# Merge of an attention layer without copies by column: stores by image, column blocks made in memory, statistics behind the next sums

## The chip, the cores and the metric

The kernel runs on one core of a Trainium2 chip. A core has TensorE (PE: matrix products, into PSUM), VectorE (DVE), ScalarE (ACT), GpSimd (POOL) and SyncE (SP, which only issues transfers), an on-chip memory of 128 partitions, and 16 DMA engines between it and the chip's main memory. SP and ACT each have a DMA queue. The metric is the time of one execution on the device, in microseconds (us).

## The reference

The input x has the shape 2 x 128 x 128 x 128 (images, channels, rows, columns; 16.8 MB in float32). Four layers follow each other, each as x = x + layer(groupnorm(x)):

- layer 0: axial attention along the rows' axis, for every column, in 8 groups, with relative position embeddings and batch normalisation of the logits and of the output;
- layer 1: four recurrent scans, down, up, right and left. A step is `y = x_i + relu(conv1d(y_prev, w))` with nine taps over 128 channels; the first two scans go over rows, the last two over columns;
- layer 2: a deformable 3 x 3 convolution;
- layer 3: a 4 x 4 convolution with stride 2, done through Hadamard transforms.

For this case the seam between layers 0 and 1 matters. Layer 1's residual is the sum x1 = x + layer0: its scans start from the normalised x1 and overwrite it, and the last scan adds the unnormalised x1 to its result.

## The kernel before, in words

*Preparation* (`layer0_prepare`). Both images are loaded to the chip (`xa`), moments of the logits are gathered, and the projected tensors are written to main memory: `v_d`, then `qa_d` from the tile `sa` and `qb_d` from `sb`. The pool `l0x` that holds the images is given memory from the left end, and so are the pools of `sa` and `sb` after it.

*Attention* (`layer0_attention`). 64 units of one image, one group and 32 columns. Its constants `toep` and its operands `zz`, `qk` and `r` are in pools at the right end. Unit 0 starts with POOL's clearing of the two `zz`, then SP loads 16 pieces of `zz`, then TensorE multiplies them with `toep` into `gen`.

*Merge* (`class Merge`). The attention's two outputs lie in main memory, `sv_d` by column and `sve_d` by row. There are 8 units (2 images of 4 blocks of 32 columns), each of two halves of 16 columns. For a half, `add` lets ACT scale and turn the columns of `tv` into `u`, in two quarters, and DVE sums them into `te`; `to_image` adds `te` to the image x in `res`, POOL the rows 0 to 63 and DVE the rows 64 to 127, and DVE takes four `bn_stats` of the result, first of its own rows, then of POOL's. `by_column` then lets ACT turn each quarter into the tile `bc` and store it, from its own queue, in `x1_d`, which holds x1 by column. SP loads `te`, `tv` and the image, each when a buffer is free. In the pools `InOrder` keeps the order of the text on an engine: ACT's is sums of this half, then columns of the half before; DVE's is sums, addition, statistics.

*Layer 1* (`layer1`). The statistics become a scale and a shift (`group_norm`); ACT starts loads for three further scan weights; `layer3_weights`, called as `prepare`, loads layer 3's weights from ACT's queue, lets POOL form sums of them and stores them from ACT's queue again. Then ACT normalises rows, four ahead of the scan. A scan step is 14 matmuls on TensorE, one ACT copy of a PSUM tile (`c0`), six DVE operations, and two ACT copies (lines 1177 and 1178) that write the new line back to the image, both images in one access. In the fourth scan POOL writes instead: `here = new + add`, where `add` is a line of x1. It comes from the tile `x1t`, eight columns of x1 by column, loaded by `load_columns` from `x1_d`, two blocks ahead. DVE takes statistics of the finished lines right after POOL's additions (`stats`).

The order of instructions on each engine is fixed when the program is built: by the text where `InOrder` is used, by a scheduler elsewhere. An instruction waits on semaphores; the DMAs of SP and ACT share eight of them in turn, so a DMA is also held until the eighth one before it has landed.

Of the kernel before, what the change touches and what calls it, by code (L numbers as in the profile page):

```python
# [15 lines left out]
P = 128  # L16
N = 2
# [74 lines left out]
def layer0_prepare(env, x, prm, mem, alphas):  # L92
# [7 lines left out]
    nc, tc = env.nc, env.tc  # L100
    HW = WC // 2
    with ExitStack() as ctx:
        xpool = ctx.enter_context(tc.tile_pool(name="l0x", bufs=1))
        kp = ctx.enter_context(tc.tile_pool(name="l0k", bufs=1))
        xa = [xpool.tile([P, S, S], F32, name=f"xa{n}", tag=f"xa{n}") for n in range(N)]
        pe, dve, act = (InOrder(tc, e) for e in (nc.tensor, nc.vector, nc.scalar))
# [782 lines left out]
class Merge:  # L889

    def __init__(self, env, x, mem, x1_d, ctx):
        self.env, self.x, self.mem, self.x1_d, self.ctx = env, x, mem, x1_d, ctx
        self.units = [(n, wc) for n in range(N) for wc in range(NC)]
        self.sums, self.embedded = {}, {}
        self.sync = InOrder(env.tc, env.nc.sync)
# [69 lines left out]
    def run(self, prm, res, mv, st_gn):  # L968
        nc, tc = self.env.nc, self.env.tc
        HWC, HS = WC // 2, S // 2  # L970
        act, dve, pool = (InOrder(tc, e) for e in (nc.scalar, nc.vector, nc.gpsimd))
        sp, units = self.sp, self.units
        with ExitStack() as ctx:
            cp = ctx.enter_context(tc.tile_pool(name="mg_c", bufs=1))
            pp = ctx.enter_context(tc.tile_pool(name="mg_ps", bufs=1, space=PSUM))
            for part in range(4):
                self.load_rows(res[0], 0, part)
            a, shift = self.scales(cp, pp, prm, mv)

            def there(at, hf):  # L980
                n, wc = units[at]
                lo = wc * WC + hf * HWC
                return res[n][:, :, lo : lo + HWC]

            HQ = HWC // 2

            def add(at, hf):

                tv = self.sums.pop((at, hf))
                for q in range(2):  # L990
                    u = sp.tile([P, S, HQ], F32, name="u", tag="u")
                    act.activation(
                        u.rearrange("p h w -> p w h"),
                        tv[:, q * HQ : (q + 1) * HQ],
                        AF.Identity,
                        bias=shift,
                        scale=a[:, 0:1],
                    )
                    lo = hf * HWC + q * HQ
                    te = self.embedded[at][:, :, lo : lo + HQ]  # L1000
                    dve.scalar_tensor_tensor(te, te, a[:, 1:2], u, ALU.mult, ALU.add)

            def to_image(at, hf):

                n, wc = units[at]
                te = self.embedded[at][:, :, hf * HWC : (hf + 1) * HWC]
                image = there(at, hf)
                for h, engine in ((0, pool), (HS, dve)):
                    here = image[:, h : h + HS, :]
                    engine.tensor_tensor(here, te[:, h : h + HS, :], here, ALU.add)  # L1010
                for b in (2, 3, 0, 1):
                    dve.bn_stats(
                        st_gn[:, n, wc * NB + hf * 4 + b, :], image[:, b * 32 : (b + 1) * 32, :]
                    )

            def by_column(at, hf):
                n, wc = units[at]
                image = there(at, hf)
                for q in range(2):
                    t = sp.tile([P, HQ, S], F32, name="bc", tag="bc", bufs=3)  # L1020
                    act.copy(t, image[:, :, q * HQ : (q + 1) * HQ].rearrange("p h w -> p w h"))
                    lo = wc * WC + hf * HWC + q * HQ
                    act.dma_start(out=self.x1_d[:, n, lo : lo + HQ, :], in_=t)

            last = None
            for at in range(len(units)):
                for hf in range(2):
                    if at > 0:  # L1030
                        add(at, hf)
                        if at + 1 < len(units):
                            self.load_sums(at + 1, hf)
                    elif hf == 0:
                        for k in range(2):
                            add(0, k)
                            self.load_sums(1, k)
                        self.load_rows(res[1], 1, 0)
                        self.load_rows(res[1], 1, 1)
                    if last is not None:  # L1040
                        by_column(*last)
                    last = at, hf
                    to_image(at, hf)
                if at + 2 < len(units):
                    self.load_embedded(at + 2)
                if at in (0, 1):
                    self.load_rows(res[1], 1, at + 2)
            by_column(*last)

# [9 lines left out]
    return wl, ws  # L1061


def layer1(env, prm, res, both, x1_d, st_gn, st_next, first, prepare):

# [1 line left out]
    nc, tc = env.nc, env.tc  # L1069
    HS = S // 2  # L1070
    with ExitStack() as ctx:
        cp = ctx.enter_context(tc.tile_pool(name="l1c", bufs=1))
        sp = ctx.enter_context(tc.tile_pool(name="l1s", bufs=3))
        with tc.tile_pool(name="l1pn", bufs=1, space=PSUM) as pn:
# [1 line left out]
        pp = ctx.enter_context(tc.tile_pool(name="l1ps", bufs=2, space=PSUM))  # L1076
        weights = [first] + [scan_weights(env, prm, cp, d) for d in range(1, 4)]
        prepare()
        xp = ctx.enter_context(tc.tile_pool(name="l1x", bufs=3))


        lines = [
# [7 lines left out]
            InOrder(tc, e) for e in (nc.tensor, nc.vector, nc.scalar, nc.gpsimd)  # L1090
        )

        CB = 8

        def load_columns(w0):
            t = xp.tile([P, N, CB, S], F32, name="x1t", tag="x1t")
            nc.sync.dma_start(out=t, in_=x1_d[:, :, w0 : w0 + CB, :])
            return t

        def stats(t, n):  # L1100
# [17 lines left out]
        for d in range(4):  # L1118
# [4 lines left out]
            for at, line in enumerate(steps):  # L1123
# [7 lines left out]
                new = [t[:, :, 2 : 2 + HS] for t in now]  # L1131
                if d == 3:
                    w0 = line // CB * CB
                    if line == w0 + CB - 1 and w0 >= 2 * CB:
                        columns[w0 - 2 * CB] = load_columns(w0 - 2 * CB)
                    add = [columns[w0][:, :, line - w0, k::2] for k in range(2)]
                if at == 0:
                    for k in range(2):
                        dve.tensor_copy(new[k], here[k])
# [588 lines left out]
def layer3_weights(env, prm, w3_d):  # L1728
# [5 lines left out]
    with tc.tile_pool(name="l3w", bufs=1) as wp:  # L1734
# [2 lines left out]
        tk = [wp.tile([P, 4, 2, H], F32, name=f"tk{k}", tag=f"tk{k}") for k in range(2)]  # L1737
        w3 = wp.tile([P, W3], F32, name="w3w", tag="w3w")
        ws, wt = layer3_views(w3)
        nc.scalar.dma_start(out=ta.rearrange("p u v o -> p (u v o)"), in_=prm["w3"])  # L1740
        pool = nc.gpsimd
        zero = wp.tile([P, 2 * P], F32, name="zero", tag="zero")
        pool.memset(zero, 0.0)
# [27 lines left out]
        for half in range(2):  # L1771
# [4 lines left out]
            if half == 1:  # L1776
                pool.tensor_tensor(to[2], y, x, sub)
                less(to[3], x, y)
        nc.scalar.dma_start(out=w3_d, in_=w3)


def layer3(env, prm, res, w3_d, st_gn, out):
# [173 lines left out]
@with_exitstack  # L1956
def program(ctx, tc, prm, out):
    nc = tc.nc
    x = prm["x"]
    cst = ctx.enter_context(tc.tile_pool(name="cst", bufs=1))  # L1960
    dram = ctx.enter_context(tc.tile_pool(name="scratch", bufs=1, space=DRAM))
    env = Env(tc, cst, prm["cst"])
    st_gn = [
        cst.tile([P, N, NT, 6], F32, name=f"st_gn{k}", tag=f"st_gn{k}") for k in range(2)
    ]
    mem = {
        "qa": dram.tile([P, N, NC, WC, S], F32, name="qa_d", tag="qa_d"),
        "qb": dram.tile([P, N, NC, 4, 4, 8, WC], F32, name="qb_d", tag="qb_d"),
        "v": dram.tile([NG, N, NC, S, WC, 16], F32, name="v_d", tag="v_d"),
        "sv": dram.tile([P, N, NC, WC, S], F32, name="sv_d", tag="sv_d"),  # L1970
        "sve": dram.tile([P, N, NC, S, WC], F32, name="sve_d", tag="sve_d"),
    }
    w3_d = dram.tile([P, W3], F32, name="w3_d", tag="w3_d")
    x1_d = dram.tile([P, N, S, S], F32, name="x1_d", tag="x1_d")
    mem["px"] = dram.tile([N, TP, TP, P], F32, name="px_d", tag="px_d")
    mem["off"] = dram.tile([N, NT, P, 4, 27], F32, name="off_d", tag="off_d")
    tables = [
        dram.tile([TE * TE, 512], F32, name=f"table{n}", tag=f"table{n}") for n in range(N)
    ]

    alphas = cst.tile([P, NG, 3], F32, name="alphas", tag="alphas")
    layer0_prepare(env, x, prm, mem, alphas)
    mv = cst.tile([P, NG, 2, 2], F32, name="mv_out", tag="mv_out")
    merging = ctx.enter_context(ExitStack())
    merge = Merge(env, x, mem, x1_d, merging)
    layer0_attention(env, prm, mem, alphas, mv, merge.begin)

    rp = ctx.enter_context(tc.tile_pool(name="res", bufs=1))
    both = rp.tile([P, N, S, S], F32, name="res", tag="res")
    res = [both[:, n] for n in range(N)]  # L1990
    with tc.tile_pool(name="l1w", bufs=1) as wp:
        first = scan_weights(env, prm, wp, 0)
        merge.run(prm, res, mv, st_gn[1])
        merging.close()
        layer1(
            env,
            prm,
            res,
            both,
            x1_d,  # L2000
            st_gn[1],
            st_gn[0],
            first,
            lambda: layer3_weights(env, prm, w3_d),
        )
    layer2(env, prm, res, mem, tables, st_gn[0], st_gn[1])
    layer3(env, prm, res, w3_d, st_gn[1], out)
# [129 lines left out]
```

## Time and profile before

| | us |
|---|---|
| runs | 5598.71, 5602.14, 5605.36 (median 5602.14) |
| the profiled execution | 5593.61 |
| its span, first to last instruction | 5591.8 |
| preparation, to the scale of the logits | to 426.1 |
| attention, to its last matmul | to 1955.0 |
| merge, to POOL's last addition | to 2121.5 |
| first matmul of the first scan | at 2158.3 |
| fourth scan | 3368 to 3785 |
| layers 2 and 3 | to the end |

A row of the timeline or of a group names the line (81 is the helper of `InOrder`), the engine, the operation and its tiles, output first; `x32` counts, and in brackets or after the bar stands how long the engine was idle before and what ended that. `ACTq` and `SPq` are DMAs issued by ACT and SP. A table by stretches has the busy time of each engine in it.

### The profile page before, as it was taken

What the parts mean: (1) busy time and instruction counts of PE and PEld (TensorE: products, weight loads), DVE (VectorE), ACT (ScalarE), POOL (GpSimd) and SP (SyncE); (2) the same over time, 40 slices, a digit from 0 to 9 for tenths busy, and PEclk for the clock granted to TensorE, in tenths of its full rate; (3) what the DMA queues carried; (4) which work ended last, traced back from release to release, by engine and by line L of the source; (5) the groups of instructions that cost most, each with busy time, mean ns of one, the idle gap of its engine ahead of it and who ended that gap; (6) DMA issues with size and microseconds to landing.
All of it is one profiled execution on the core that took longest, in us unless ns stands there. A gap on an engine that the chain in (4) does not pass through costs nothing. (4 is left out here: it accounts for less than half of the span.)

```text
span 5591.8 us, 171680 instructions
## 1 busy us (share of the span) xinstructions
PE 5225.9 (93%) x71931; PEld 4654.5 (83%) x71931; DVE 3684.3 (66%) x7132; ACT 2642.4 (47%) x7896; POOL 1531.2 (27%) x1169
## 2 busy tenths in 40 slices
PE   7997999999999805999999999999899999999999
PEld 6866888888888705999999999994699999999877
DVE  3635888888888764555555556664466666666798
ACT  1056989889888774443223331003233333333322
POOL 2114666666666632000000002330000000000376
PEclk8998999999999957999999999999999999999999
DMA  3353333333333392000000000103577676677111
GB/s 152 107 220 84 61 60 60 60 62 63 60 60 62 95 389 100 1 1 1 1 1 1 1 1 31 47 24 112 117 89 86 89 87 90 88 88 87 45 50 58
DMA packets 413993, 404.21 MB, mean 72 GB/s; under 512 B 63521, under 2 KB 368545, under 8 KB 402337
## 3 DMA queue, kind: packets, MB, share of 16 engines
q1 hardware_dynamic: 403150, 364.77, 31.7%
q10 hardware_dynamic: 10066, 28.36, 1.4%
q8 instruction: 576, 9.44, 0.7%
q14 instruction: 201, 1.64, 0.1%
HBM read 252.31 MB, written 140.68 MB: 70 GB/s over the span
## 5 line engine op out<-in xcount | busy, mean ns | idle before, releaser
L81 PE MATMUL pl<-ln,wl 128*128 128x128 f32 (+1 forms) x10160 | 1239.5, 276 | 30.7 <-DVE ln L81 30.7
L81 PEld LDWEIGHTS pl<-ln,wl 128*128 128x128 f32 x10160 | 1176.3, 190 | 41.6 <-issue 27.3
L81 ACT ACTIVATE e<-e,mx 128x128 f32<-128x128 f32 x2048 | 793.4, 395 | 0.8 <-DVE mx L81 0.8
L81 ACT COPY sm<-ps_s 128x432 f32<-128x432 f32 (+1 forms) x768 | 318.4, 487 | 831.7 <-PE ps_s L81 808.4
L81 POOL TENSOR_TENSOR e<-e,total 128x1024 f32<-128x1024 f32 x256 | 485.6, 1897 | 474.4 <-DVE total L81 462.8
L81 ACT COPY res<-ln 128x128 f32<-128x128 f32 x762 | 261.8, 344 | 722.0 <-DVE ln L81 722.0
L81 DVE COPY s<-ps_w 100x1152 f32<-100x1152 f32 x256 | 346.5, 1354 | 331.9 <-PE ps_w L81 331.9
L81 PE MATMUL ps_s<-s,xw 100*128 100x144 f32 x4096 | 546.4, 287 | 5.4 <-DMA xw<-px_d 5.4
L81 POOL TENSOR_TENSOR res<-ln,x1t 128x128 f32<-128x128 f32 x256 | 133.9, 523 | 1494.6 <-DVE ln L81 1494.6
L81 PE MATMUL po<-sm,wdef 128*128 128x256 f32 x2304 | 539.2, 379 | 0.0
L81 PE MATMUL pl<-ln,ws 128*128 128x128 f32 x4064 | 536.8, 273 | 0.0
L81 POOL COPY et<-et 128x1024 f32<-128x1024 f32 x256 | 516.9, 2019 | 34.9 <-DVE et L81 25.8
L81 PEld LDWEIGHTS ps_s<-s,xw 100*128 100x128 f32 x4096 | 518.2, 190 | 5.9 <-issue 5.8
L81 DVE TENSOR_TENSOR v<-pl,c 128x128 f32<-128x128 f32 x508 | 148.2, 292 | 538.3 <-PE pl L81 538.3
L81 PEld LDWEIGHTS pl<-ln,ws 128*128 128x128 f32 x4064 | 494.5, 190 | 0.0
L81 ACT ACTIVATE r<-gen,alphas 128x1536 f32<-128x1536 f32 x256 | 395.0, 1543 | 174.1 <-PE gen L81 144.0
L81 PEld LDWEIGHTS po<-sm,wdef 128*128 128x128 f32 x2304 | 419.8, 190 | 47.7
L81 POOL MEMSET col<- 128x10 f32 (+1 forms) x72 | 5.9, 122 | 1459.6 <-DVE res L81 1452.1
L81 ACT ACTIVATION_READ_ACCUMULATOR e<-e,mx 128x1 f32 x2048 | 396.5, 194 | 0.0
L81 DVE SCALAR_TENSOR_TENSOR ln<-v,res 128x128 f32<-128x128 f32 x1016 | 343.7, 338 | 49.2 <-DVE v L81 1.2
L81 PE MATMUL te<-cst_main,e 128*128 128x128 f32 x2048 | 337.0, 287 | 25.7 <-POOL e L81 18.0
L81 PE MATMUL gen<-zz,toep 32*128 32x128 f32 x8192 | 333.1, 288 | 24.5 <-DMA zz<-qb_d 17.0
(245 smaller groups left out, 9222.5 us busy)
## 6 DMA issues: line engine op xcount, KB each, us to landing
xw<-px_d SPq DMA_DIRECT2D x1275, 80.0 KB
xa<-in_x SPq DMA_DIRECT2D x16, 1024.0 KB
v_d<-vs SPq DMA_DIRECT2D x16, 1024.0 KB
qb_d<-sb SPq DMA_DIRECT2D x16, 1024.0 KB
qa_d<-sa SPq DMA_DIRECT2D x8, 2048.0 KB
zz<-qb_d SPq DMA_DIRECT2D x1024, 16.0 KB
vt<-v_d SPq DMA_DIRECT2D x64, 256.0 KB
qk<-qa_d SPq DMA_DIRECT2D x256, 64.0 KB
```

What stands on the lines that cost most here:

```text
L81: return lambda *a, **k: self.tc.keep_in_program_order(issue(*a, **k))
```

## The change

- Preparation's images (`l0x`) are given memory from the right end.
- `by_column` is gone: no turned copies, no stores in the merge.
- In the merge, `to_image` no longer takes statistics. DVE takes those of its own rows after its addition, and those of POOL's rows after the next half's sums. `u` has four buffers instead of two.
- Layer 1 begins with stores of the image rows to `x1_d`, which now holds x1 by row: pieces of 4, then 8, at the end 4 rows, of each image, on SP.
- Eight copies from `x1_d` to the new `x1c_d`, on SP, gather 16 columns each, in runs of 16 elements. `load_columns` reads `x1c_d`, blocks of 16 columns instead of 8, two buffers instead of three; POOL reads its line from them at a step of 32 elements.
- Load and store of layer 3's weights are issued by SP instead of ACT.

```diff
-        xpool = ctx.enter_context(tc.tile_pool(name="l0x", bufs=1))
+        xpool = ctx.enter_context(tc.tile_pool(name="l0x", bufs=1, side="right"))
...
-                    u = sp.tile([P, S, HQ], F32, name="u", tag="u")
+                    u = sp.tile([P, S, HQ], F32, name="u", tag="u", bufs=4)
...
-                for b in (2, 3, 0, 1):
+
+            def stats(at, hf, half):
+                n, wc = units[at]
+                image = there(at, hf)
+                for b in (2 * half, 2 * half + 1):
                     dve.bn_stats(
                         st_gn[:, n, wc * NB + hf * 4 + b, :], image[:, b * 32 : (b + 1) * 32, :]
                     )
 
-            def by_column(at, hf):
-                n, wc = units[at]
-                image = there(at, hf)
-                for q in range(2):
-                    t = sp.tile([P, HQ, S], F32, name="bc", tag="bc", bufs=3)
-                    act.copy(t, image[:, :, q * HQ : (q + 1) * HQ].rearrange("p h w -> p w h"))
-                    lo = wc * WC + hf * HWC + q * HQ
-                    act.dma_start(out=self.x1_d[:, n, lo : lo + HQ, :], in_=t)
...
                     if last is not None:
-                        by_column(*last)
+                        stats(*last, 0)
                     last = at, hf
                     to_image(at, hf)
+                    stats(at, hf, 1)
...
-            by_column(*last)
+            stats(*last, 0)
...
     with ExitStack() as ctx:
+        for lo, hi in [(0, 4)] + [(h, h + 8) for h in range(4, S - 4, 8)] + [(S - 4, S)]:
+            for n in range(N):
+                nc.sync.dma_start(out=x1_d[:, n, lo:hi, :], in_=res[n][:, lo:hi, :])
...
-        xp = ctx.enter_context(tc.tile_pool(name="l1x", bufs=3))
+        xp = ctx.enter_context(tc.tile_pool(name="l1x", bufs=2))
...
-        CB = 8
+        CB = 16
+        for k in range(S // CB - 1, -1, -1):
+            nc.sync.dma_start(
+                out=x1c_d[k].rearrange("p n h w -> p (n h) w"),
+                in_=x1_d.rearrange("p n h w -> p (n h) w")[:, :, k * CB : (k + 1) * CB],
+            )
 
         def load_columns(w0):
-            t = xp.tile([P, N, CB, S], F32, name="x1t", tag="x1t")
-            nc.sync.dma_start(out=t, in_=x1_d[:, :, w0 : w0 + CB, :])
+            t = xp.tile([P, N, S, CB], F32, name="x1t", tag="x1t")
+            nc.sync.dma_start(out=t, in_=x1c_d[w0 // CB])
             return t
...
-                    if line == w0 + CB - 1 and w0 >= 2 * CB:
-                        columns[w0 - 2 * CB] = load_columns(w0 - 2 * CB)
-                    add = [columns[w0][:, :, line - w0, k::2] for k in range(2)]
+                    if line == w0 + CB - 1 and CB <= w0 < S - CB:
+                        columns[w0 - CB] = load_columns(w0 - CB)
+                    add = [columns[w0][:, :, k::2, line - w0] for k in range(2)]
...
-        nc.scalar.dma_start(out=ta.rearrange("p u v o -> p (u v o)"), in_=prm["w3"])
+        nc.sync.dma_start(out=ta.rearrange("p u v o -> p (u v o)"), in_=prm["w3"])
...
-        nc.scalar.dma_start(out=w3_d, in_=w3)
+        nc.sync.dma_start(out=w3_d, in_=w3)
...
+    x1c_d = dram.tile([8, P, N, S, 16], F32, name="x1c_d", tag="x1c_d")
```

More of the change, by code (lines that the diff above doesn't have):

```diff
@@ L889, with __init__ @@
 class Merge:
-    def __init__(self, env, x, mem, x1_d, ctx):
-        self.env, self.x, self.mem, self.x1_d, self.ctx = env, x, mem, x1_d, ctx
+    def __init__(self, env, x, mem, ctx):
+        self.env, self.x, self.mem, self.ctx = env, x, mem, ctx
         self.units = [(n, wc) for n in range(N) for wc in range(NC)]
@@ L1061, in scan_weights, with layer1 @@
     return wl, ws
-def layer1(env, prm, res, both, x1_d, st_gn, st_next, first, prepare):
+def layer1(env, prm, res, both, x1_d, x1c_d, st_gn, st_next, first, prepare):
     nc, tc = env.nc, env.tc
@@ L1984, in program @@
     merging = ctx.enter_context(ExitStack())
-    merge = Merge(env, x, mem, x1_d, merging)
+    merge = Merge(env, x, mem, merging)
     layer0_attention(env, prm, mem, alphas, mv, merge.begin)
@@ L2000, in program @@
             x1_d,
+            x1c_d,
             st_gn[1],
```

## The prediction

> **What bounds the kernel now.** The chain of waits stops after 8 us at the end of the program (its shares are all 0%), so I read the stages in order of time instead: first the slices of the page, which show one stretch where the DMA engines are full and TensorE is idle.
>
> ```profile
> DMA  3353333333333392000000000103577676677111
> GB/s 152 107 220 84 61 60 60 60 62 63 60 60 62 95 389 100 1 1 1 1 1 1 1 1 31 47 24 112 117 89 86 89 87 90 88 88 87 45 50 58
> ```
>
> A slice is 140 us. Slice 15 (1957 to 2097) is the merge; slices 17 to 24, three of the four scans, move almost nothing. The table by stretches (length, then busy us of PE, PEld, DVE, ACT and POOL, granted clock, DMA share, GB/s) cuts the merge and what follows it:
>
> ```profile
> 1960.00:2045.00 85.00, 0.00 (x0) 0.00 (x0) 44.55 (x51) 53.63 (x28) 21.99 (x7) 0.50 1.01 421
> 2045.00:2105.00 60.00, 0.00 (x0) 0.00 (x0) 44.01 (x49) 53.64 (x28) 24.14 (x7) 0.50 0.98 354
> 2105.00:2130.00 25.00, 0.00 (x0) 0.00 (x0) 14.43 (x17) 18.27 (x10) 7.20 (x3) 0.50 0.41 156
> 2130.00:2160.00 30.00, 2.25 (x10) 2.22 (x11) 3.66 (x18) 3.18 (x9) 20.87 (x28) 0.50 0.34 130
> ```
>
> Full DMA and a nearly full ACT (107 of 145 us) share the merge; in 2130:2160 no engine but POOL works. The groups of 1960:2130, costliest first (busy us, mean ns, idle before):
>
> ```profile
> L81 ACT ACTIVATE u<-tv,shift,a_out 128x1024 f32<-128x1024 f32 x32 | 67.4, 2213 | 17.6 <-DMA tv<-sv_d 11.1 <-ACT bc L81 5.5 <-DVE shift L965 1.0
> L81 ACT COPY bc<-res 128x1024 f32<-128x1024 f32 x32 | 61.0, 1906 | 23.5 <-DVE res L81 14.3 <-ACT bc L81 5.2 <-DMA x_d<-bc 3.0
> L81 POOL TENSOR_TENSOR res<-te,res 128x1024 f32<-128x1024 f32 x16 | 53.0, 3316 | 121.3 <-DVE te L81 96.9 <-DMA res<-in_x 24.5
> L81 DVE SCALAR_TENSOR_TENSOR te<-te,a_out,u 128x1024 f32<-128x1024 f32 x32 | 41.1, 1285 | 34.6 <-ACT u L81 34.6
> L81 DVE BATCH_NORM_STATS2 st_gn<-res 128x6 f32<-128x512 f32 x64 | 41.0, 685 | 14.3 <-POOL res L81 13.7
> L81 DVE TENSOR_TENSOR res<-te,res 128x1024 f32<-128x1024 f32 x16 | 19.6, 1224 | 12.2 <-DMA res<-in_x 11.7
> ```
>
> The timeline then shows what stands between the merge and the first scan's first copy back:
>
> ```profile
> 2125.82 0.33 ACTq L81 DMA_DIRECT2D x_d<-bc  x1
> ...
> 2128.76 1.90 DVE L54 BATCH_NORM_AGGREGATE mv_l<-st_gn 128x2 f32<-128x192 f32 x2 [5.96 <-DMA x_d<-bc]
> ...
> 2156.64 0.33 ACTq L1779 DMA_DIRECT2D w_d<-w3w  x1
> 2157.03 4.72 ACT L81 ACTIVATE res<-res,gb_l,gs_l 128x128 f32<-128x128 f32 x12 [24.07 <-POOL w3w L1751]
> ...
> 2163.33 0.31 ACT L81 COPY res<-ln 128x128 f32<-128x128 f32 x1 [1.43 <-DVE ln L81]
> ```
>
> The last column store is awaited for its memory, and then ACT stands 24 us: the store of layer 3's weights is queued ahead of the normalisation and waits for POOL. Last, the start of attention:
>
> ```profile
> 434.34 3.54 POOL L613 MEMSET zz<- 128x2048 f32 x2 [11.95 <-DMA qb_d<-sb]
> 436.17 6.03 SPq L81 DMA_DIRECT2D zz<-qb_d  x16
> ...
> 440.14 1.61 PE L81 MATMUL gen<-zz,toep 32*128 32x128 f32 x4 [15.82 <-DMA zz<-qb_d]
> ...
> ```
>
> [...] POOL's addition takes 2.4 us alone (4.77 us for two at 1971.61) and 3.45 us when DVE's addition (1.23 us) starts just before it. [...] the loads of zz land behind the stores issued before them. [...] Here the first 20 matmuls after the merge took 4.48 us and the next 20 2.40.
>
> **The change, part by part.**
>
> *Merge.* Gone are 32 ACT copies (61.0 us) and their 16.8 MB of stores. ACT keeps 67 us, loads alone run at 421 GB/s, so neither is the bound of its later half. A half unit on DVE is 2 x 1.285 + 1.224 + 4 x 0.645 (1.29 us per pair) = 6.4 us. Now DVE's order changes: statistics of rows 0 to 63 follow the next sums instead of preceding them. This removes their wait for POOL (13.7 us in all before), but POOL's addition now starts when the sums end, under those statistics [...]: 2.3 us, of which 1.29 pass under the statistics, and DVE's own addition waits about 1.0 us. A half unit becomes 7.4 us; with no such wait it is 6.4. At first loads bound it: from 1985 the queue holds 4.2 MB of image 1, 2.1 of te, 2.1 of image and 2.1 of tv (10.5 MB at 0.42 MB/us, so unit 2 sums from about 2010), then 5.2 MB up to unit 3's first tv (2023.5). Unit 3 waits 4.4 us for its two u and ends at about 2042. Seven of the eight half units left take 7 x 7.4 = 52, the last one's sums 2.6 and POOL's addition 2.3: it ends at about 2099 (2091 without the wait, 2101 if sums wait as well). Before, it ended at 2121.5. Gain to here 22 us.
>
> *Stores by image.* In the changed program's order SP issues rows 0 to 51 of image 0 (3.4 MB, 8.4 us) after the last tv load, that is under the merge's end; the next is image 1's rows 0 to 3, which wait for POOL's last addition, and all others stand behind it. From there 24 stores of 4 KB rows and 3 of 2 KB rows remain: an engine moves 8 packets of each, at 159 ns (4096 bytes) and 84 ns (2048) in this trace's packet records, 24 x 1.27 + 3 x 0.67 = 32.5 us. Three weights of 576 KB interleave (8 x 178 ns each, 4.3 us). With 0.85 us from issue to first packet and 0.6 to the waiter, the store before the last lands 37 us after POOL's last addition: 2136. Who waits? Normalising row 0 waits only for the first pieces and starts at about 2105. But the first copy back into the image (both images in one access, the ACT copies of line 1178) waits in the changed order for the last store of image 0. ACT is in order, so the next step's c copy stands behind it: the scan takes one step and stops until 2136. That is the new wait in place of the two removed.
>
> *Weights of layer 3.* Load and store go from ACT's to SP's queue, so ACT no longer waits for POOL's 17 us of sums (24.07 us of stall). The load lands behind the image stores, POOL's sums run some 20 us under the first scan, and layer 3 alone needs them. SP waits meanwhile, with only seven column copies behind it; its 34 new issues (0.33 us each) are under the transfers. Cost 0; without that cover it is the 24 us again.
>
> *Sum of merge and scan start.* Before, the second step's c copy came at 2165.36; after, at 2136 + 1.55 (two copies and two normalisations first). The array has by then idled 25 us and pays its 2.1 us of half clock again. 2165.4 - 2137.6 - 2.1 = 25.7 us gained; 18 to 34 by the ends above and stores at 354 instead of 410 GB/s.
>
> *Column copies.* Eight DRAM copies of 32,768 runs of 64 bytes: 16,384 descriptors for each of 16 engines. No packet of 64 bytes is in the trace; 96-byte packets take 12 ns, 216-byte ones 18, 432-byte 25, 512-byte 53 (median; 29 in a clean 1 MB store). Bounds 12 to 53 ns, I take 20: 330 us, at most 870. They start at 2137 (one) and 2158 (seven) and lie under three scans with idle queues. The loads of x1t stand behind all eight in the ring and are needed at about 3350, when the fourth scan's first statistics wait for POOL: seven copies fit if a descriptor costs under 83 ns. Cost taken: 0. POOL's additions read x1t at a step of 128 bytes instead of 8; DVE's like access went from 294 to 383 ns with a larger step, and POOL is busy 133 of 415 us there, so 0.
>
> *Image at the other end.* The memory of zz and toep is no longer under sa and sb, whose stores end at about 433: POOL's clearing runs early and zz's loads are queued behind the stores at once. But the seventh and eighth of 16 wait for ve's load and the last store (about 436), and the other eight are issued at 0.38 us: last landing 441.5 against 443.6. Gain 2 us (-1 to 6).
>
> **Sum.** 25.7 + 2 = 28 us off the profiled execution's 5593.6 us (span 5591.8), 5566. The median of the runs shown is 8.5 us higher, 5602.1; the same difference gives 5574, or 0.5% less.
>
> **Rivals.** [...] DVE's half unit stays at 6.4, all is 8 us earlier, 5566. For it: 0.58 against 0.47 us is all that POOL loses to DVE in the fourth scan. *Stores gate later*: mixed with loads the DMA fell to 354 GB/s; the 37 us become 43[...]: 5583 to 5590, half of it near nothing. *Slower*: the column copies miss the fourth scan. Place: x1t's first load behind all eight copies. Decides at 83 ns per descriptor; at 100 ns they end at 3592, 240 us late, so 5815. Against it: nothing in the trace under 512 bytes comes near; for it, no DRAM to DRAM copy is there. *Copies disturb the scans*: each 14 us an instruction fetch of 16 KB passes the same engines (29 in 400 us); a us lost at each over 330 us costs 24, to 5598.
>
> **Chances.** Forecast 0.54, [...] later gate 0.14, late copies 0.10, disturbed scans 0.08. A measurement can tell 0.2%, 11 us. Faster: 0.54 + 0.14 + 0.09 + 0.03 = 0.80; same 0.05 + 0.03 = 0.08; slower 0.10 + 0.02 = 0.12. Range 5558 to 5596, which leaves out the late copies and the tails; the likeliest case alone spans 5566 to 5584.
>
> **What would show it.** Merge: POOL's last addition at 2091 to 2101, DVE's addition near 2.2 us instead of 1.22. Gate: an ACT copy back idle some 25 us on DMA x1_d, ending near 2136. Step times of the first three scans unchanged (3.13 us). x1t's first loads landing before 3340. Wrong if the image stores finish elsewhere, if scan steps lengthen under the copies, or if a fourth-scan addition waits on DMA.

## The result, and the profile after

The changed kernel takes 5575.55 us (median of 6 runs, 5574.42 to 5577.40), the kernel before 5598.18 us in the six runs beside it (5596.62 to 5605.36). The ratio is 0.9957, with a 95% interval from 0.9945 to 0.9970: 22.6 us faster, where 28 were forecast. The profiled execution has a span of 5574.0 us against 5591.8.

The line of the page with the GB/s of each slice (139 us now). Slice 15, the merge, has fallen from 389 to 338; slices 16 and 17 hold the image stores and the column copies, and what follows of the first three scans again moves almost nothing:

```profile
GB/s 152 108 221 85 60 60 60 60 60 61 60 60 63 95 338 186 100 1 1 1 1 1 1 1 32 47 16 119 113 87 89 88 85 88 90 88 88 44 50 58
```

The same table by stretches (length, busy us of PE, PEld, DVE, ACT and POOL with their counts, granted clock, DMA share, GB/s):

```profile
1960.00:2045.00 85.00, 0.00 (x0) 0.00 (x0) 57.34 (x65) 40.70 (x21) 19.18 (x8) 0.50 0.92 374
2045.00:2105.00 60.00, 0.00 (x0) 0.00 (x0) 59.72 (x60) 25.52 (x13) 19.53 (x9) 0.50 0.73 285
2105.00:2130.00 25.00, 9.40 (x58) 9.18 (x58) 6.24 (x24) 5.19 (x14) 3.81 (x3) 0.64 1.03 419
2130.00:2160.00 30.00, 18.65 (x131) 17.93 (x132) 12.35 (x30) 9.14 (x30) 16.96 (x24) 0.72 1.53 200
```

In 2045:2105 DVE is busy for 59.72 of 60 us and the DMA share has fallen from 0.98 to 0.73: DVE is now the bound of the merge's later half. The full DMA has moved to 2105:2130, where it holds the image stores, and TensorE works there for 9 us and stops. The groups of 1960:2130, cut to those that the forecast priced (busy us, mean ns, idle before):

```profile
L81 DVE BATCH_NORM_STATS2 st_gn<-res 128x6 f32<-128x512 f32 x64 | 40.8, 682 | 0.6
...
L81 POOL TENSOR_TENSOR res<-te,res 128x1024 f32<-128x1024 f32 x16 | 38.4, 2402 | 112.7 <-DVE te L81 87.9 <-DMA res<-in_x 24.8
L81 DVE TENSOR_TENSOR res<-te,res 128x1024 f32<-128x1024 f32 x16 | 36.8, 2297 | 11.8 <-DMA res<-in_x 11.8
```

The statistics no longer wait for POOL (0.6 us of idle instead of 14.3), POOL's addition takes 2.40 us instead of 3.32, and DVE's own 2.30 on average instead of 1.22 (2.45 in the 14 of 16 beside which POOL adds). The timeline shows what the first scan then meets (ACT normalises, ACT copies back, POOL begins layer 3's sums, a DVE step operation beside them):

```profile
2108.96 4.72 ACT L81 ACTIVATE res<-res,gb_l,gs_l 128x128 f32<-128x128 f32 x12 [0.43 <-DVE gb_l L69]
...
2138.91 0.50 ACT L81 COPY res<-ln 128x128 f32<-128x128 f32 x2 [24.95 <-DMA x_d<-res]
...
2143.04 4.89 POOL L1767 TENSOR_TENSOR tb<-ta 128x256 f32<-128x256 f32 x7 [29.44 <-DMA ta<-in_w]
...
2147.59 0.49 DVE L81 SCALAR_TENSOR_TENSOR ln<-v,res 128x128 f32<-128x128 f32 x1
```

POOL's last addition ends at 2099.90 instead of 2121.48 and ACT normalises at 2108.96 instead of 2157.03. Then the first copy back stands 24.95 us for an image store: among the semaphores that it waits for, that of image 0's last store (the last but one in all) comes last, at 2138.77. This wait is called the gate in what follows. Behind it stands the second step's c copy (ACT's copy of a PSUM tile, one in each step), at 2140.10 instead of 2165.36. Of the 48 us by which the normalisation is earlier, 25 are left at this copy. The column copies are seen by their tile: from 2139.5 SP issues them, most of them held for some 25 us at the queue (shortest, middle and longest issue in ns).

```profile
L1095 SPq DMA_DIRECT2D x1c_d<-x_d x8: 483/25527/27906, 2139.5 to 2295.9; - x8
```

Their 262,144 packets of 64 bytes take 19 ns each in the median and are done at 2348, 1000 us before the fourth scan.

**Where the time went, stage by stage.** The stretch before the merge varies more between executions than some of the parts studied here: the merge's first ACT activation lies anywhere from 1954.5 to 1966.2 in the eleven traces of this study. So from here on stages are counted from that activation (1960.22 before, 1962.16 after).

| us from the merge's first activation | before | after | difference |
|---|---|---|---|
| POOL's last addition ends | 161.3 | 137.7 | -23.5 |
| second step's c copy | 205.1 | 177.9 | -27.2 |
| eleven steps later | 239.5 | 216.6 | -22.9 |
| end of the first scan (its last c copy) | 595.5 | 575.0 | -20.5 |
| end of the fourth scan | 1821.5 | 1800.4 | -21.1 |
| end | 3631.6 | 3611.8 | -19.8 |

Of 27.2 us won at the second step's c copy, 6.7 are given back within the first scan, 4.3 of them in the next eleven steps.

### The profile page after: what moved, and what is told of

Read it like the earlier page. It is cut to its first block, busy times and chain, and to the rows that moved or that the text cites. A ratio compares the mean times of both kernels' runs of the same rounds, so it can differ in the third digit from the quotient of the medians.

```text
span 5574.0 us, 171601 instructions
## 1 busy us (share of the span) xinstructions
PE 5231.2 (94%) x71931; PEld 4656.9 (84%) x71931; DVE 3700.6 (66%) x7132; ACT 2582.8 (46%) x7864; POOL 1532.4 (27%) x1169
## 5 line engine op out<-in xcount | busy, mean ns | idle before, releaser
L81 POOL TENSOR_TENSOR res<-ln,x1t 128x128 f32<-128x128 f32 x256 | 149.1, 583 | 1456.0 <-DVE ln L81 1456.0
L81 POOL COPY et<-et 128x1024 f32<-128x1024 f32 x256 | 516.8, 2019 | 34.9 <-DVE et L81 25.7
L81 DVE COPY et<-te 128x512 f32<-128x512 f32 x512 | 348.3, 680 | 13.3 <-PE te L81 13.0
```

Of the source, the lines that this page charges most:

```text
L81: return lambda *a, **k: self.tc.keep_in_program_order(issue(*a, **k))
```

## The experiments

**The weights' move alone.**

```diff
--- the kernel before
+++ the kernel before, layer 3's weights on SP
-        nc.scalar.dma_start(out=ta.rearrange("p u v o -> p (u v o)"), in_=prm["w3"])
+        nc.sync.dma_start(out=ta.rearrange("p u v o -> p (u v o)"), in_=prm["w3"])
...
-        nc.scalar.dma_start(out=w3_d, in_=w3)
+        nc.sync.dma_start(out=w3_d, in_=w3)
```

> The kernel before with one edit only: the load and the store of layer 3's weights go from ACT's queue to SP's. Theory (the 24.07 us that ACT stood behind that store were the last wait before the first scan, and nothing in the kernel before stands ready to take its place): the second step's c copy comes 22 to 24 us earlier, at about 2142 instead of 2165.36, POOL's sums then run under the first steps and lengthen five to seven of them by 0.3 to 0.5 us each (2 to 3 us in all), and the time is 20 to 22 us below before, about 5577, which is all of what the whole change brought. Rival (the gain of the change comes from the merge and the stores, as the sum of the prediction has it, 22 us of its 28): this edit alone brings little, because another wait takes over, and the time stays within 8 us of 5598.

Measured: 5578.95 us against 5602.93 of the kernel before beside it, ratio 0.9960 (0.9947 to 0.9974). From the merge's first activation the c copy comes after 182.7 us (22.4 earlier) and the end after 3610.9, 0.9 us before that of the whole change. The 24 us wait is gone from ACT's timeline; the normalisation now follows the statistics at once:

```profile
2138.63 4.72 ACT L81 ACTIVATE res<-res,gb_l,gs_l 128x128 f32<-128x128 f32 x12 [0.48 <-DVE gb_l L69]
```

Two changed queue names bring what the whole change brings: the two ratios can't be told apart. The rest of the change, with its merge 23.5 us shorter, nets to nothing beside them.

**The change without the weights' move.**

```diff
--- the changed kernel
+++ the changed kernel, layer 3's weights back on ACT
-        nc.sync.dma_start(out=ta.rearrange("p u v o -> p (u v o)"), in_=prm["w3"])
+        nc.scalar.dma_start(out=ta.rearrange("p u v o -> p (u v o)"), in_=prm["w3"])
...
-        nc.sync.dma_start(out=w3_d, in_=w3)
+        nc.scalar.dma_start(out=w3_d, in_=w3)
```

> The changed kernel with the load and the store of layer 3's weights put back on ACT's queue. Theory (in the changed kernel the image stores hold the first copy back until 2138.9 anyway, and ACT's wait for POOL's sums ends before that or with it): ACT stands until about 2132, the second step's c copy stays at 2138 to 2143, the steps after it are not lengthened by POOL any more, and the time is within 4 us of the changed kernel's 5575.6. Rival (the prediction's words: without that cover it is the 24 us again): about 5599.

Measured: 5582.54 us, ratio 0.9965 (0.9951 to 0.9979). That is 7 us above the changed kernel, neither within the expected 4 us nor 24. The five runs lie 11 us apart, so the count from the merge's first activation says more: the end is 9.4 us later (3621.2). ACT stands 26.3 us and normalises at 2134.86, but the copy back, which was to be free at about 2139, comes at 2150.84. The waits of SP in this stretch (total, times, longest) tell why, and the timeline its effect:

```profile
SPq L1071 <- DMA w_d<-w3w: 14.2, 1, 14.2
```

```profile
2134.86 4.72 ACT L81 ACTIVATE res<-res,gb_l,gs_l 128x128 f32<-128x128 f32 x12 [26.27 <-POOL w3w L1756]
...
2150.84 0.50 ACT L81 COPY res<-ln 128x128 f32<-128x128 f32 x2 [11.10 <-DMA x_d<-res]
```

An image store on SP stood 14.2 us for the weights' store on ACT's queue. They share no data: in the trace both name the same semaphore (104), since the DMAs of both queues take eight semaphores in turn (100 to 105, 107 and 108) and each waits until the one before it on its semaphore has landed. So ACT's wait for POOL reached SP's stores and the DMA engines fell partly idle (144 GB/s in 2130:2140, 390 in the changed kernel). The price of eight semaphores for two queues is seen here as these 14.2 us.

**Image 0's stores first.**

```diff
-        for lo, hi in [(0, 4)] + [(h, h + 8) for h in range(4, S - 4, 8)] + [(S - 4, S)]:
-            for n in range(N):
+        for n in range(N):
+            for lo, hi in [(0, 4)] + [(h, h + 8) for h in range(4, S - 4, 8)] + [(S - 4, S)]:
                 nc.sync.dma_start(out=x1_d[:, n, lo:hi, :], in_=res[n][:, lo:hi, :])
```

> The changed kernel with the loops of the image stores exchanged: all rows of image 0, then all rows of image 1. Theory (the first copy back waits for the last store of image 0 only because its two images' access is guarded as one stretch from row 0 of image 0 to row 0 of image 1): image 0's stores are done by about 2104, image 1's first rows soon after POOL's last addition at 2099.9, so the 24.95 us wait of the copy back is gone, the second step's c copy comes at about 2117.4 instead of 2140.1, the second start at half clock (2.1 us) is saved too, and the time is 5551 (5546 to 5556). Rival (the stores as a whole set the end, whatever their order, because the copies back of later rows wait for image 1's stores or for the column copies): the wait only moves to a later step and the time stays at 5570 to 5577.

Measured: 5556.06 us, ratio 0.9915 (0.9902 to 0.9929); 3590.6 us from the merge's first activation, 21.2 less than the changed kernel. The bytes, the transfers and the engines' work are the same; only the order of 34 stores differs. The wait of the copy back is gone:

```profile
2117.50 4.34 ACT L81 ACTIVATE res<-res,gb_l,gs_l 128x128 f32<-128x128 f32 x11 [3.24 <-DMA x_d<-res]
...
2123.41 0.31 ACT L81 COPY res<-ln 128x128 f32<-128x128 f32 x1 [1.42 <-issue]
```

So the stores as such did not set the end; what did was the guard of a copy that touches row 0 of both images and was held for all that image 0 still had to store. The expected 5551 was missed by 5 us; its five runs lie between 5547.9 and 5561.0. Counted from the merge's first activation, the c copy was expected after 155 us and came after 159.3. A cause is in SP's waits before and during these stores:

```profile
SPq L1071 <- DMA wl<-in_wscan: 10.8, 2, 10.2
```

Image 0's stores stood 10.2 us for loads of scan weights on ACT's queue, which ACT can issue only when the merge has ended, and which take their turn in the same eight semaphores. In the changed kernel the same waits come to 4.0 us. The last experiment below takes this wait away.

**The statistics at once.** `stats(at, hf, 0)` directly behind `stats(at, hf, 1)`, as in the kernel before, and no statistics behind the next sums:

```diff
-                    if last is not None:
-                        stats(*last, 0)
-                    last = at, hf
                     to_image(at, hf)
                     stats(at, hf, 1)
+                    stats(at, hf, 0)
...
-            stats(*last, 0)
```

> The changed kernel with the merge's statistics all right after the addition, as in the kernel before (rows 64 to 127, then 0 to 63), and so no statistics behind the next sums. Theory [...]: DVE's addition falls from 2.30 to about 1.25 us, POOL's rises from 2.40 to about 3.4, DVE waits about 1 us per half unit for POOL, a half unit stays at 7.2 to 7.5 us, POOL's last addition ends within 3 us of 2099.9, and the time within 3 us of the changed kernel. Rival (the order is worth the 13.7 us that DVE waited for POOL in the kernel before): the merge ends 7 to 14 us later and the time is 5582 to 5590.

Measured: 5575.39 us, ratio 0.9955 (0.9941 to 0.9968), the time of the changed kernel; POOL's last addition ends 138.4 us after the merge's first activation (137.7), the end is at 3612.5 (3611.8). The groups of 1960:2130:

```profile
L81 POOL TENSOR_TENSOR res<-te,res 128x1024 f32<-128x1024 f32 x16 | 53.0, 3316 | 99.7 <-DVE te L81 73.9 <-DMA res<-in_x 25.8
L81 DVE BATCH_NORM_STATS2 st_gn<-res 128x6 f32<-128x512 f32 x64 | 41.0, 684 | 14.3 <-POOL res L81 13.7
```

DVE's addition is back at 1224 ns, POOL's at 3316, and the 13.7 us of waiting for POOL are there again, and the merge takes no longer for it. In the changed order DVE's additions take 16 x (2297 - 1224) ns = 17.2 us more instead: one wait is exchanged for another. Moving the statistics behind the next sums is worth nothing here. The merge's 23.5 us come from the removed column copies together with the four `u` buffers; these two were not tried apart.

**One more DVE instruction.**

```diff
         for pair in lines:
             for t in pair:
                 nc.vector.memset(t, 0.0)
+        nc.vector.memset(lines[0][0], 0.0)
```

> The changed kernel with one more small instruction on DVE (a second clearing of the first line buffer) ahead of the first scan. In the changed kernel's first scan every sixteenth step is 0.34 us longer (0.23 and 0.11), also when no DMA runs any more; the late instruction is DVE's first addition of the step, which starts 0.41 us after its semaphore instead of 0.06, and DVE has 8 instructions in a step, so 128 in sixteen. The kernel before has one DVE instruction more ahead of the scan and no such steps there. Theory [...]: the seven long steps of the first scan vanish (2.4 us), and the second, third and fourth scans take the lengths of the kernel before (395.2, 405.0 and 411.8 us instead of 394.0, 404.4 and 413.1). Rival (the column copies or the memory's layout lengthen these steps): the pattern stays at steps 18, 34, 50 and so on.

Measured (a single execution, 5567.78 us): the seven long steps are gone, and the second to fourth scans take 395.2, 404.9 and 411.7 us, the lengths of the kernel before. The end is at 3608.5 us from the merge's first activation (3611.8); 2.1 of these 3.3 us are the scans', and the length of layers 2 and 3 differs by up to 1.4 us among the traces. In the trace of the changed kernel a usual and a long step, by DVE's first addition, look like this (the idle before it in brackets):

```profile
2194.87 0.29 DVE L81 TENSOR_TENSOR v<-pl,c 128x128 f32<-128x128 f32 x1 [1.14 <-PE pl L81]
...
2198.34 0.29 DVE L81 TENSOR_TENSOR v<-pl,c 128x128 f32<-128x128 f32 x1 [1.49 <-PE pl L81]
```

0.35 us more pass before the same instruction. Long steps come every sixteen steps, and DVE's queue holds eight instructions in a step (six operations and two that only wait), so 128 in sixteen. Within 4.2 us of the start of each long step a packet of 8192 bytes of an instruction queue follows (2201.7, 2252.1, 2302.4 and so on, after steps that start at 2197.5, 2247.9 and 2298.3). Whose instructions it carries, and whether it holds the step up, no trace shows. Shown is that the long steps go with one instruction more.

**The column copies twice.**

```diff
-        for k in range(S // CB - 1, -1, -1):
+        for k in [k for k in range(S // CB - 1, -1, -1) for _ in range(2)]:
             nc.sync.dma_start(
```

> The changed kernel with each of the eight column copies made twice: 32,768 descriptors of 64 bytes for each engine instead of 16,384. Theory (the copies cost nothing because three scans cover them, at 12.6 ns per descriptor and engine): the copies end at about 2555 instead of 2348, the steps of the first scan stay at 3.13 us where they are 3.13 in the changed kernel, the fourth scan finds its first columns in time, and the profiled span stays within 3 us of the changed kernel's 5574.0. Rival (the copies lengthen the scan's steps, which is where some of the 6.8 us came from that the first scan lost after its restart): the first scan becomes 2 to 7 us longer.

Measured (a single execution): span 5573.0 us, 3611.5 from the merge's first activation. The copies end at 2557, (2557 - 2140) us / 32,768 = 12.7 ns per descriptor and engine, and the first scan has the same steps, long ones included (358.4 us from the thirteenth step's c copy to its last one in both). Copies under the scans cost nothing, also when there are twice as many.

**The image at its old end.**

```diff
-        xpool = ctx.enter_context(tc.tile_pool(name="l0x", bufs=1, side="right"))
+        xpool = ctx.enter_context(tc.tile_pool(name="l0x", bufs=1))
```

> The changed kernel with the image of the preparation at its old end of memory. Theory (the prediction's: 2 us gained by the move): the first r of attention comes at 446 to 447 us instead of 444.80, and POOL's clearing of zz waits for the last store of sb again. Rival (the move is worth nothing that can be told): the first r lies anywhere between 440.4 and 446.7, which is how far it differs among the changed kernel and three variants of it whose first 440 us are the same code.

Measured (a single execution, 5568.70 us): the first r of attention comes at 442.06 us, the merge's first activation at 1954.46, the earliest of all traces. With the image at the right end that r comes at 437.6 to 446.7 in eight traces, so its time alone tells nothing. Counted from SP's issue of the last store of `sb`, which all versions have, it does: the first r follows after 23.8, 25.2 and 24.5 us in the three traces with the image at the left end (the kernel before, the weights' move alone, this run) and after 21.4 to 23.4 us in the eight others. The means are 24.5 and 22.4. In the three POOL's clearing waits for that store (12.6 us in this run); in the eight it begins before the store is issued, as in the changed kernel:

```profile
420.13 1.81 POOL L613 MEMSET zz<- 128x2048 f32 x1 [1.16 <-PE ps_q L81]
```

So the move gains about 2 us at its place. The time of the whole can't show it: from this r to the merge's first activation it takes between 1512 and 1522 us, whichever end the image has.

**Image 1's first piece from ACT's queue.** With image 0's stores first and the one DVE instruction more:

```diff
+                queue = nc.scalar if (n, lo) == (1, 0) else nc.sync
-                nc.sync.dma_start(out=x1_d[:, n, lo:hi, :], in_=res[n][:, lo:hi, :])
+                queue.dma_start(out=x1_d[:, n, lo:hi, :], in_=res[n][:, lo:hi, :])
```

> The changed kernel with image 0's stores first, with image 1's first piece (rows 0 to 3) stored from ACT's queue, and with the one DVE instruction more. Theory (with image 0's stores first, the next wait at the scan's start is the 3.24 us of the second normalisation for image 1's first piece, which stands behind image 0's stores on SP's queue; and the periodic long steps can be moved out of the way): both add up, 3 us and 2 us off the 5556 of image 0's stores first, so about 5551, with the second step's c copy at about 2122 instead of 2125.5. Rival (the copies back wait for image 0's last stores at about the same time, so the wait only changes its name): 5554 to 5557.

Measured: 5552.30 us, ratio 0.9921 (0.9907 to 0.9934), between the two forecasts. The second normalisation no longer waits, but the tenth does (4.59 us for an image store), and the c copy comes 159.8 us after the merge's first activation, as late as without the edit (159.3). So the rival's account held: the wait changed its name. Of the two gains only that of the DVE instruction came (3589.2 us to the end against 3590.6). The longest wait of SP's stores was 8.2 us, for the piece on ACT's queue, again through a shared semaphore (105):

```profile
SPq L1072 <- DMA x_d<-res: 24.1, 13, 8.2
```

**The scans' weights on SP, behind the stores.** With image 0's stores first and the one DVE instruction more:

```diff
-    nc.scalar.dma_start(out=wl, in_=prm["wscan"][:, d])
+    (nc.sync if d else nc.scalar).dma_start(out=wl, in_=prm["wscan"][:, d])
```

> The changed kernel with image 0's stores first, with the loads of the scans' weights 1 to 3 moved from ACT's queue to SP's, behind the image stores, and with the one DVE instruction more. Theory (with image 0's stores first, SP stood 10.2 us for the weights' loads, because those loads, which ACT can issue only when the merge has ended, take their turn in the same semaphores as the stores; the piece stored from ACT's queue made the same wait, 8.2 us): SP has no such wait, image 0's stores end before the merge does, the second normalisation and the ninth to tenth wait for no store, and from the merge's first activation to the second step's c copy it takes 154 to 156 us instead of 159.3 (image 0's stores first) and 159.8 (first piece from ACT's queue); the whole from there to the end 3584 to 3586 us instead of 3590.6 and 3589.2. Rival (the stores of image 0 are bound by the DMA engines, which also load the last units): the c copy stays at 159 us.

Measured: 5546.46 us, ratio 0.9905 (0.9889 to 0.9922); the c copy after 154.8 us and the end after 3585.5, both as expected; the DVE instruction alone leaves the c copy where it is (177.8 us against 177.9). In SP's waits nothing of ACT's queue is left. The stores still wait for earlier transfers of their own queue, each for at most 3.2 us, and for what they really need, the merge's last addition:

```profile
SPq L1071 <- POOL res L81: 2.8, 1, 2.8
```

This is the fastest version found, 54 us (1.0%) below the kernel before.

## Why the prediction was right, and where it was not

**The total** (5574 forecast, 5575.55 measured) is closer than its parts, and that is luck. The forecast took 28 us off a median of 5602.1; six runs put the kernel before at 5598.2 and the gain at 22.6. So its start was 3.9 us too high and its gain 5.4 us too large, and the two nearly cancel. That the profiled execution of the kernel before stood 8.5 us below the runs shown was mostly chance: that of the changed kernel (5575.76) lies 0.2 us above its median.

**Merge: right.** POOL's last addition was put at 2099 and ended at 2099.90; DVE's addition was put near 2.2 us and took 2.30, with DVE busy throughout the later half. The sum let the statistics' new order save the wait for POOL and pay about as much in DVE's addition (the last one starts 1.03 us after POOL's, at 2098.52, and takes 2.45 us instead of 1.22), and the run with the statistics at once shows this exchange. The first rival (chance 0.14) is refuted: it put a half unit at 6.4 us, and the last ones took 7.26 (DVE's additions start at 2091.26 and 2098.52), where 7.4 was forecast.

**Stores by image: right in mechanism, 2 us short.** The first copy back waits for image 0's last store, ACT's next c copy stands behind it, and the scan takes one step and stops. The gate was forecast at 37 us after POOL's last addition (its own terms add up to 37.6) and opened at 39.0. The sum has the scan weights' bytes, but not the 4.0 us that SP stood for them through shared semaphores. The run with these loads on SP shows that such waits count; how much of the 2 us they are is not shown.

**Weights of layer 3, cost 0: wrong by 2 us.** The step hid POOL's sums under the first scan. But in the merge already an addition of one took longer beside that of the other (POOL's 3.45 us instead of 2.40 in the kernel before, DVE's 2.45 instead of 1.22 now), and there the prediction counted it. Beside the sums `ln<-v,res` takes up to 0.80 us and `ln<-ln,ln` up to 0.70 instead of 0.29, and a step 3.58 us instead of 3.13; with the weights back on ACT the sums end before the scan, and no operation there is longer. In the changed kernel this (about 2.2 us) and the second start at half clock (about 2.1 us, which the prediction had in its sum: with 0.50 granted in 2140:2145 the first 20 matmuls took 4.64 us, the next 20 2.52) make the 4.3 us lost in the eleven steps after the gate. Wrong too was that without this cover "it is the 24 us again". It is 7 to 9, since the gate hides most of it. Most of those arise from the shared semaphore: the first step's c copy comes at 2139.49, and with the 3.7 us from there to the second that the kernel before has, the second would come at about 2143. That is an estimate from these two traces; it came at 2152.02.

**Not in the sum at all:** the seven long steps of the first scan, 2.4 us. The steps of the first three scans were called unchanged; the other three scans differ by 0.6 to 1.3 us, and one DVE instruction more gives all four their old lengths.

**Image at the other end, 2 us: right.** From the last store of `sb` to the first r it is 2.1 us less (means of eight and three traces). In the time of the whole this drowns in the spread before the merge.

**Column copies: right.** 12.6 ns per descriptor instead of 20, end at 2348; POOL's addition with the wider step takes 557 ns in the median instead of 497 and costs nothing: with one more DVE instruction the fourth scan has its old 411.7 us. *Late copies* and *disturbed scans* are refuted, the latter by the doubled copies.

**What the prediction did not see** is how its parts stand to one another. It worked out one sum for all of them, 25.7 us with the half clock in it. Measured were 27.2 us at the c copy, so 25.1 less the half clock's 2.1, then 22.9 after the steps beside POOL's sums, 20.5 after the long steps and 19.8 at the end. But it asked of no part what it would bring alone. The runs show two waits behind each other before: the merge, and ACT's 24 us. Removing ACT's wait alone is worth 20.7 us (3631.6 - 3610.9), all the rest alone 10.4 (3631.6 - 3621.2, with the shared semaphore's wait in it), both together 19.8, because the new gate takes the place of both. With the gate gone it is 41.0 (3631.6 - 3590.6).

## What to carry to other kernels

Before a rebuilt stage is credited with a gain, look for the one wait at its seam that a smaller edit removes, and time that edit alone: here two changed queue names were worth as much as the whole change. When several transfers guard one access, order them so that the access's whole guarded stretch is done first; when two queues share semaphores, put nothing that waits for compute into one of them while the other has a stream to keep going (14.2 us here). And work put under a loop as free still has to be checked against each of that loop's own operations: beside POOL's sums a step took 3.58 us instead of 3.13.

## What the runs showed of the hardware that was not expected

- A DMA on one queue stood 14.2, 10.2 and 8.2 us for one on the other queue with which it shared only a semaphore, while the DMA engines had room: they moved 144, 293 and 268 GB/s in 10 us within or around each wait (2130:2140, 2100:2110, 2090:2100 of their traces), and about 420 when full.
- A DRAM to DRAM copy in runs of 64 bytes took 12.6 ns per descriptor and engine (83 GB/s moved in all from 2200 to 2300), with eight copies standing in one queue. The scan beside it kept its length when there were twice as many (358.4 us in both).
- One small instruction ahead of a loop moved the four scans by -2.4, +1.2, +0.5 and -1.4 us; the first scan's long steps, 0.35 us each, come once in sixteen steps of eight DVE instructions.
